# Layer 1's attention: transposing the probabilities one row of scores later

## The chip, the cores and the metric

The kernel runs on one core of a Trainium2 chip. Its engines work side by side, each through its own queue of instructions: TensorE (PE in the profile; its weight loads are listed as PEld), VectorE (DVE), ScalarE (ACT), GpSimd (POOL) and SyncE (SP, which here only issues transfers). The metric is the device time of one execution in microseconds (us); lower is better.

## The reference

Four layers, each of which adds an attention-like part and a feed-forward part to the residual x. All is float32. The change is in layer 1's attention, a latent attention with 16 heads over 4 sequences of 512 tokens. Cut to what matters:

```python
q = _rmsnorm(x @ wq_a, q_a_ln_w) @ wq_b              # 16 heads of 128 + 64
ckv = x @ wkv_a                                       # 64 latent + 64 rotary
kv = _rmsnorm(compressed_kv, kv_a_ln_w) @ wkv_b
q_pe, k_pe = rotary(q_pe), rotary(k_pe)
scores = jnp.einsum('bqhd,bkhd->bhqk', qf, kf) * softmax_scale
scores = jnp.where(causal, scores, finfo.min)
attn = jax.nn.softmax(scores, axis=-1)
out = jnp.einsum('bhqk,bkhd->bqhd', attn, v).reshape(b, s, -1) @ wo
...
x = x + _L1_attn_ref(xn, ...) + _L1_ffn_ref(xn, ...)
```

Layer 1's feed-forward part is a product-key lookup (512 experts, 8 gathered for each token) plus a gated MLP of width 1024.

## The kernel before

**Streams woven together.** A layer is written as several Python generators. Each emits some instructions and then yields an estimate of what they cost; `weave` always resumes the generator that is least advanced in relation to its total. In layer 1 these are the attention (`latent_pieces`, total 457), the product-key lookup (237, mostly DVE, POOL gathers and ACT), the gated MLP (126, mostly PE) and, from late on, the first part of layer 2. The framework then schedules the woven program: the order written is a priority, and an instruction that its estimate takes to be ready may be issued ahead of one that is not. Instructions wrapped in `keep_in_program_order` are pinned behind the previous one written for the same engine. The framework also adds all semaphores, and lets a tile wait until the buffer it reuses is free.

**The attention.** One step `s` of the loop stands for one head of one sequence; there are 64, and two neighbours make a pair. Each has four rows of scores, `i` = 0 to 3, of 128 queries against 128, 256, 384 and 512 keys (the causal half).

- `probabilities(s, i)` emits one row: the score matmul (L1042, two instructions), the masked reduction on DVE (L1045), the exponential on ACT with its row sum (L1049). After row 2 the sums of rows 0 to 2 are inverted on DVE (L1165) and the three rows scaled on ACT (L1167), after row 3 the last row. The rows `pr0` to `pr3` have two buffers each.
- `turned(s, j)` emits piece j of the transposed probabilities (L1174): the blocks of key block j from rows j to 3, so 4, 3, 2 and 1 transposes on PE, into a PSUM bank of the tag "tr", which has two banks. The copy out of the bank into `PT` (L1178) is returned as a function, and emitted after the next piece: on DVE for j = 0 and 2 (512 and 256 columns), on ACT for j = 1 and 3 (384 and 128). `PT` has two buffers, one for each head of a pair.
- The values' product `z` of a pair of heads (L1328): 16 matmul calls of 64 output rows, pinned in order, which read both heads' `PT`. ACT copies it scaled to `zT` (L1334, three buffers).
- `out_pieces` (L1282): after every second pair, the product with the output weights, in two pieces, which are emitted after row 1 and row 3 of the next odd step, and added to x on DVE (L212).
- `queries(p)` (L1129 to L1134, and with new weights of a group of heads L1103 to L1117) emits the next pair's projected queries at row 0 of an even step, with the exchange of halves through four transfers `psw<-pes` on SP (L1139). `rotate` (L1148 to L1151) emits their rotation on DVE at row 0 of an odd step.

PSUM has four banks of tag "mm" (scores, projections, the MLP), two of "tr", and two of "acc" (z, output products).

In source order, step s emits for each i: score row i of head s, transposes T(i) of head s - 1, copy of T(i - 1). At the end of the step comes the last copy, and at the end of an even step z of the pair s - 2, s - 1. So with the row number in brackets:

```
odd s:   row(0) T(0) | row(1) T(1) out | row(2) T(2) | row(3) T(3) out
even s:  row(0) T(0) queries | row(1) T(1) | row(2) T(2) | row(3) T(3) z
```

where the output pieces stand only in every fourth step. Step 64 has no scores and finishes the last pair.

Of the kernel before, what the change touches and what calls it, by code (L numbers as in the profile page):

```python
# [16 lines left out]
P = 128  # L17
NB, SEQ, DM = 4, 512, 256
NT = NB * SEQ
NTILE = NT // P  # L20
TPB = SEQ // P
# [1013 lines left out]
def exp_scores(c, pool, late, q, k, i, total, scale=1.0, kept=lambda ins: ins, **kw):  # L1035

    nc = c.nc
    n = (i + 1) * P  # L1040
    sc = c.ps()[:, :n]
    kept(nc.tensor.matmul(sc, lhsT=q[:, i * P : n], rhs=k[:, :n], start=True, stop=True))  # L1042
    pr = c.tile(pool, [P, n], f"pr{i}", **kw)
    nm = c.tile(pool, [P, 1], "nm", bufs=4)
    nc.vector.tensor_tensor_reduce(  # L1045
        out=pr, in0=sc, in1=late[:, SEQ - n :], scale=scale, scalar=-NEG,
        op0=ALU.add, op1=ALU.min, accum_out=nm,
    )
    nc.scalar.activation(pr, pr, AF.Exp, bias=nm, scale=-1.0, accum_out=total)  # L1049
    return pr  # L1050
# [20 lines left out]
def latent_pieces(c, a, keep, open_pool):  # L1071
# [20 lines left out]
    pool = open_pool()  # L1092
    weights = {}

    def carry(g):

        w = c.unit(a["l_units"][g])
        wqT, wkT, wvT = v3(w[:, :768], QL), v3(w[:, 768:1024], KL), v3(w[:, 1024:1280], KL)
        wo = v3(w[:, 1792:2816], DM)
        pw, pv = c.ps(), c.ps()  # L1100
        for h in range(4):
            hk = slice(h * KL, (h + 1) * KL)
            nc.tensor.matmul(pw[:, hk], lhsT=wqT[:, h, :P], rhs=wkT[:, h, :], start=True, stop=True)  # L1103
            nc.tensor.matmul(
                pv[(h % 2) * KL : (h % 2 + 1) * KL, (h // 2) * DM : (h // 2 + 1) * DM],
                lhsT=wvT[:, h, :], rhs=wo[:, h, :], start=True, stop=True,
            )
        pw1 = c.ps()
        for h in range(4):
            hk = slice(h * KL, (h + 1) * KL)  # L1110
            nc.tensor.matmul(pw1[KL:, hk], lhsT=wqT[:, h, P:], rhs=wkT[:, h, :], start=True, stop=True)
        wl0 = c.tile(pool, [P, 256], "wl0")
        wl1 = c.tile(pool, [P, 256], "wl1")
        wz = c.tile(pool, [P, 2, DM], "wz")
        nc.scalar.copy(wl0, pw[:, :256])
        nc.scalar.copy(wl1[KL:, :], pw1[KL:, :256])
        nc.scalar.copy(wz, v3(pv, DM))  # L1117
        weights[g] = w[:, 1280:1536], w[:KL, 1536:1792], wl0, wl1, wz

    def queries(p):  # L1120

        g, b, pair = p // 8, p // 2 % 4, p % 2
        if p % 8 == 0:
            carry(g)
        wpe0, wpe1, wl0, wl1, _ = weights[g]
        tokens = slice(b * SEQ, (b + 1) * SEQ)
        cols = slice(pair * P, (pair + 1) * P)
        pe, pl = c.ps(), c.ps()
        nc.tensor.matmul(pl, lhsT=wl0[:, cols], rhs=qa0[:, tokens], start=True, stop=False)  # L1129
        upper = nc.tensor.matmul(pe, lhsT=wpe1[:, cols], rhs=qa1[:KL, tokens], start=True, stop=False)  # L1130
        with tc.issue_after(upper.ins), tc.high_priority(offset=200):
            nc.tensor.matmul(pl, lhsT=wl1[KL:, cols], rhs=qa1[KL:, tokens], start=False, stop=True)
        with tc.high_priority(offset=100):
            nc.tensor.matmul(pe, lhsT=wpe0[:, cols], rhs=qa0[:, tokens], start=False, stop=True)  # L1134

        pes, psw = (c.tile(pool, [P, SEQ], n, bufs=1) for n in ("pes", "psw"))
        nc.scalar.copy(pes, pe)
        for to in range(0, P, 32):
            nc.sync.dma_start(psw[to : to + 32, :], pes[to ^ 32 : (to ^ 32) + 32, :])  # L1139
        qf = c.tile(pool, [P, 2, SEQ], "qf")  # L1140
        nc.scalar.mul(qf[:KL, 0, :], pl[:KL, :], -scale)
        nc.scalar.mul(qf[KL:, 1, :], pl[KL:, :], -scale)
        qfs[p] = qf
        return pes, psw, qf

    def rotate(pes, psw, qf):
        pec = c.tile(pool, [P, SEQ], "pec", bufs=1)
        nc.vector.tensor_mul(pec, pes, cosq)  # L1148
        tc.keep_in_program_order(nc.vector.tensor_mul(psw, psw, sinq))
        nc.vector.tensor_add(qf[:KL, 1, :], pec[:KL, :], psw[:KL, :])  # L1150
        nc.vector.tensor_add(qf[KL:, 0, :], pec[KL:, :], psw[KL:, :])  # L1151

    def probabilities(s, i):
        p, h = s // 2, s % 2
        b = p // 2 % 4
        if i == 0:
            totals[s] = c.tile(pool, [P, TPB], "total")
        rinv = totals[s]
        prs[s].append(exp_scores(
            c, pool, late, qfs[p][:, h, :], kf[:, h, b * SEQ : (b + 1) * SEQ], i, rinv[:, i : i + 1]  # L1160
        ))
        if i >= TPB - 2:

            done = slice(0, i + 1) if i < TPB - 1 else slice(i, i + 1)
            nc.vector.reciprocal(rinv[:, done], rinv[:, done])  # L1165
            for j in range(TPB)[done]:
                nc.scalar.mul(prs[s][j], prs[s][j], rinv[:, j : j + 1])  # L1167

    def turned(s, j):

        pt = c.ps("tr")
        n = SEQ - j * P
        for i in range(j, TPB):
            nc.tensor.transpose(  # L1174
                pt[:, (i - j) * P : (i - j + 1) * P], prs[s][i][:, j * P : (j + 1) * P], c.ident
            )
        copy = nc.scalar.copy if j % 2 else nc.vector.tensor_copy
        return lambda: copy(PTs[s][:, START[j] : START[j] + n], pt[:, :n])  # L1178

    START = (0, 512, 896, 1152)  # L1180
    qfs, prs, totals, PTs, zTs = {}, {}, {}, {}, {}
# [84 lines left out]
    turning = queries(0)  # L1266
# [8 lines left out]
    def out_pieces(g, b):  # L1275

        wz, parts = weights[g][4], zTs.copy()
        for t in range(0, TPB, 2):
            po = v3(c.ps("acc"), DM)
            for j in range(2):  # L1280
                for k in range(2):
                    nc.tensor.matmul(  # L1282
                        po[:, j, :], lhsT=parts[k][:, (t + j) * P : (t + j + 1) * P],
                        rhs=wz[:, k, :], start=(k == 0), stop=(k == 1),
                    )
            add_pair(c, b * TPB + t, po)
            if g == 3 and t == TPB - 2:
                c.part_done(b)
            yield 1.7

    copy, pieces = None, iter(())
    yield 1.9
    for s in range(65):
        if s < 64:
            prs[s] = []
        for i in range(TPB):
            if s < 64:
                probabilities(s, i)
            if s > 0:
                if i == 0:  # L1300
                    PTs[s - 1] = c.tile(pool, [P, 1280], "PT")
                ready, copy = copy, turned(s - 1, i)
                if ready:
                    ready()
            if i == 0 and s % 2 == 1 and s < 63:
                rotate(*turning)
            yield 0.85
            if i % 2:
                yield from islice(pieces, 1)
            if i == 0 and s % 2 == 0 and s < 62:  # L1310
                turning = queries(s // 2 + 1)
                yield 2.6
        if copy:
            copy()
            copy = None
        if s > 0:
            del prs[s - 1]
        if s % 2 == 1:
            continue
        if s == 0:  # L1320
            continue

        p = s // 2 - 1
        g, b, pair = p // 8, p // 2 % 4, p % 2
        z = c.ps("acc")
        for j in range(TPB):
            for h in range(2):
                tc.keep_in_program_order(nc.tensor.matmul(  # L1328
                    z[h * KL : (h + 1) * KL, j * P :], lhsT=cv[:, b * TPB + j, :],
                    rhs=PTs[s - 2 + h][:, START[j] : START[j] + SEQ - j * P],  # L1330
                    start=(j == 0), stop=(j == TPB - 1),
                ))
        zTs[pair] = c.tile(pool, [P, SEQ], "zT", bufs=3)
        nc.scalar.mul(zTs[pair], z, kv_w)  # L1334
        yield 2.1
        if pair == 1:
            pieces = out_pieces(g, b)
# [1176 lines left out]
```

## Time and profile before

| what | value |
|---|---|
| time, median of 3 runs | 2913.95 us (2909.5 to 2915.22) |
| the profiled execution | 2915.69 us |
| its span, first to last instruction | 2913.9 us |
| mean granted TensorE clock | 0.996 |
| layer 1's heads, first transposes to last | 857 to 1457 us |
| in these 600 us: PE busy | 582.8 us, with 2703 matmul instructions |
| PEld, DVE, ACT, POOL busy | 340.6, 486.6, 410.3, 120.8 us |
| transposes L1174 | 640 instructions, 124.9 us busy |
| scalings L1167 on ACT | 256, 123.5 us |
| copies L1178 on DVE and on ACT | 128 of 550 ns and 128 of 361 ns |

All times inside an execution are microseconds from the first instruction. In a group line, "x4" counts instructions, and in brackets stands how long the engine was idle before and what released it. Matmuls are pipelined: the recorded duration of one overlaps the next, so PE's busy time says little about how densely it works, and the distance from start to start says more. A line number is that of the instruction in the listing above.

### The profile page before, as it was taken

To read this page: it belongs to the slowest core of one execution; us is meant where nothing else is said; L and a number is where in the kernel's file an instruction comes from. 1 tells how busy PE (TensorE), PEld (TensorE's weight loads), DVE (VectorE), ACT (ScalarE), POOL (GpSimd) and SP (SyncE) were. 2 spreads that over 40 slices of the span, in tenths; PEclk is the share of its full clock that TensorE was granted. 3 is DMA by queue.
4 is the path that set the end of the run, shared out by engine and by line. 5 is a ranking of instruction groups with operands and counts; after the bars stand their busy time and mean duration, and the time that the engine had idled before them with its cause. 6 is when DMAs were issued, how large, how long until landed. Compare 5 with 4: busy or idle time off the path is not lost.

```text
span 2913.9 us, 40511 instructions
## 1 busy us (share of the span) xinstructions
PE 2860.2 (98%) x13767; PEld 1920.8 (66%) x13767; DVE 2131.7 (73%) x5421; ACT 1401.9 (48%) x3354; POOL 862.4 (30%) x687
## 2 busy tenths in 40 slices
PE   9999999999999999999999999999999999999999
PEld 5566665666655655555577688888888756666666
DVE  6778778787778787888775687777777666666666
ACT  4444445454366666667733554444444333333332
POOL 0565655656510033333035100000000043333331
PEclk9999999999999999999999999999999999999999
DMA  2433333333320144444234544444444300000000
GB/s 106 119 109 115 113 98 95 109 116 97 109 82 17 54 101 124 116 107 112 79 120 120 164 118 125 144 130 130 147 124 141 102 1 22 22 22 22 22 1 30
DMA packets 138687, 268.60 MB, mean 92 GB/s; under 512 B 19729, under 2 KB 99105, under 8 KB 134129
## 3 DMA queue, kind: packets, MB, share of 16 engines
q1 hardware_dynamic: 124016, 218.20, 24.4%
q0 software_dynamic: 14176, 47.04, 6.5%
q8 instruction: 109, 1.79, 0.3%
q14 instruction: 98, 0.79, 0.1%
q10 hardware_dynamic: 288, 0.79, 0.1%
HBM read 202.25 MB, written 54.26 MB: 88 GB/s over the span
## 4 chain that ended last, share of the span: by engine, by line
PE 59%; DVE 7%; ACT 4%; DMA 2%; issue 1%; SPq 0%; POOL 0%; DVEq 0%; ACTq 0%
PE mm L358 17%; PE acc L358 7%; PE mm L1042 6%; PE tr L358 6%; PE acc L1709 5%; PE acc L1058 4%; PE mm L177 3%; PE acc L266 1%; PE acc L1328 1%; DVE pr L1045 1%; PE tr L1174 1%; ACT pr L1049 1%; PE mm L185 1%; PE mm L2121 1%; ACT pr L1167 1%
## 5 line engine op out<-in xcount | busy, mean ns | idle before, releaser
L1049 ACT ACTIVATE pr<-pr,nm 128x128 f32<-128x128 f32 (+3 forms) x512 | 286.4, 560 | 297.6 <-DVE nm L1045 293.4
L1045 DVE CUSTOM_DVE_ANT_0 pr<-mm,late 128x128 f32<-128x128 f32 (+3 forms) x512 | 246.0, 483 | 115.9 <-PE mm L1042 114.3
L177 PE MATMUL mm<-xnT,wu 128*128 128x512 f32 x624 | 283.2, 595 | 0.9 <-DVE cy L620 0.5
L369 ACT COPY part<-mm 128x512 f32<-128x512 f32 (+1 forms) x372 | 177.9, 479 | 210.8 <-PE mm L358 202.6
L358 PE MATMUL mm<-token_sums,unit_sums 128*128 128x512 f32 (+1 forms) x624 | 268.1, 512 | 3.6 <-ACT part L369 3.6
L1435 POOL DMA_INDIRECT e<-in_p_experts,ids x128 | 127.7, 998 | 463.7 <-DVE x L206 358.3
L177 PE MATMUL mm<-xnT,w_in 128*128 128x512 f32 x512 | 230.9, 594 | 2.8 <-DVE cy L620 2.8
L520 DVE SCALAR_TENSOR_TENSOR x<-acc,cw,x 128x128 f32<-128x128 f32 x372 | 128.7, 346 | 106.8 <-PE acc L358 105.1
L177 PEld LDWEIGHTS mm<-xnT,wu 128*128 128x128 f32 x624 | 115.4, 190 | 126.6 <-issue 117.9
L620 DVE SCALAR_TENSOR_TENSOR cy<-mm,ws,cy 128x509 f32<-128x509 f32 (+2 forms) x216 | 159.8, 744 | 40.9 <-ACT cy L616 37.1
L1042 PE MATMUL mm<-kf,qf 128*128 128x128 f32 (+3 forms) x512 | 180.2, 443 | 3.8 <-DVE nm L1045 1.9
L785 ACT ACTIVATE xD<-xc,ws 128x128 f32<-128x128 f32 x256 | 83.6, 390 | 193.3 <-POOL y L826 182.8
L802 POOL TENSOR_TENSOR G<-G,CB 128x1024 f32<-128x1024 f32 x64 | 151.1, 2361 | 76.8 <-DVE G L765 76.8
L1042 PE MATMUL mm<-k,q 128*128 128x128 f32 (+3 forms) x512 | 170.5, 438 | 2.6 <-DVE nm L1045 2.3
L358 PEld LDWEIGHTS acc<-down_sums,hidden_sums 128*128 128x128 f32 x744 | 111.7, 191 | 85.1 <-issue 83.4
L177 PEld LDWEIGHTS mm<-xnT,w_in 128*128 128x128 f32 x512 | 95.8, 190 | 107.2 <-issue 91.8
L1709 PEld LDWEIGHTS acc<-PT,V 128*128 128x128 f32 x1280 | 153.8, 193 | 5.1 <-issue 1.7
L1709 PE MATMUL acc<-PT,V 128*128 128x128 f32 x1280 | 153.9, 276 | 0.0
L302 POOL TENSOR_TENSOR down_sums<-wu 128x256 f32<-128x256 f32 x8 | 5.8, 730 | 498.4 <-DMA wu<-in_o_units 498.4
L765 DVE TENSOR_TENSOR_SCAN G<-G,eye 128x1024 f32<-128x1024 f32 x64 | 147.2, 2300 | 0.1
L1174 PEld LDWEIGHTS tr<-con,pr 128*128 128x128 f32 x640 | 82.3, 141 | 89.9 <-ACT pr L1167 26.7
L503 DVE TENSOR_TENSOR whole<-mm,part 128x512 f32<-128x512 f32 x128 | 88.5, 692 | 68.9 <-PE mm L358 68.9
(456 smaller groups left out, 6735.1 us busy)
## 6 DMA issues: line engine op xcount, KB each, us to landing
turned<-Y SPq DMA_DIRECT2D x252, 160.0 KB, 2.6
PT<-turned SPq DMA_DIRECT2D x63, 640.0 KB, 3.9
G<-own SPq DMA_DIRECT2D x64, 512.0 KB, 4.7
w_in<-in_m_units SPq DMA_DIRECT2D x16, 1024.0 KB, 5.9
eb<-since SPq DMA_DIRECT2D x96, 128.0 KB, 3.5
wu<-in_o_units SPq DMA_DIRECT2D x6, 1536.0 KB, 6.6
wo<-in_m_units SPq DMA_DIRECT2D x16, 512.0 KB, 4.3
psw<-pes SPq DMA_DIRECT2D x128, 64.0 KB, 2.0
```

The lines of the kernel that those rows point to most:

```text
L177: c.nc.tensor.matmul(out, lhsT=w[:, d, cols], rhs=c.xnT[:, d, tokens], start=(d == 0), stop=(d == 1))
L358: self.kept(self.c.nc.tensor.matmul(bank, lhsT=lhsT, rhs=rhs, start=first, stop=True, skip_group_check=not first))
L369: self.c.nc.scalar.copy(r, bank)
L520: c.nc.vector.scalar_tensor_tensor(x, bank, self.factor(u, tt), x, ALU.mult, ALU.add)
L620: nc.vector.scalar_tensor_tensor(y[:, j:], src[:, : SEQ - j], conv[:, k, 3 - j : 4 - j], y[:, j:], ALU.mult, ALU.add,)
L765: tc.keep_in_program_order(nc.vector.tensor_tensor_scan(flat, flat, eye.rearrange("p h t -> p (h t)"), 0.0, ALU.mult, ALU.add))
L802: nc.gpsimd.tensor_mul(G, G, seqs[b][2][:, t, :][:, None, :].to_broadcast([P, HG, P]))
L1042: kept(nc.tensor.matmul(sc, lhsT=q[:, i * P : n], rhs=k[:, :n], start=True, stop=True))
L1045: nc.vector.tensor_tensor_reduce(out=pr, in0=sc, in1=late[:, SEQ - n :], scale=scale, scalar=-NEG, op0=ALU.add, op1=ALU.min, accum_out=nm,)
L1049: nc.scalar.activation(pr, pr, AF.Exp, bias=nm, scale=-1.0, accum_out=total)
L1435: nc.gpsimd.indirect_dma_start(out=e, out_offset=None, in_=a["p_experts"], in_offset=bass.IndirectOffsetOnAxis(ap=ids[:, t, k : k + 1], ax ...
L1709: kept(nc.tensor.matmul(zs[:, i], lhsT=head["V"][:, j, h, :], rhs=head["PT"][:, :, i * (i + 1) // 2 + j, :], start=(j == 0), stop=(j == i),))
```

## The change

The loop over heads and rows is flattened: n counts rows of scores, s = n // 4 and i = n % 4. A row of scores is emitted at its n as before. Piece j of head `done` is emitted at n = 4 done + j + 5 instead of 4 done + j + 4: one row of scores later. The values' product of a pair follows its last piece, as before, and so now comes after row 0 of the next odd step instead of at the end of the even one. Queries, rotation and output pieces keep their places among the rows.

```diff
-    for s in range(65):
+    for n in range(4 * 65 + 1):
+        s, i = divmod(n, TPB)
         if s < 64:
-            prs[s] = []
-        for i in range(TPB):
-            if s < 64:
-                probabilities(s, i)
-            if s > 0:
-                if i == 0:
-                    PTs[s - 1] = c.tile(pool, [P, 1280], "PT")
-                ready, copy = copy, turned(s - 1, i)
-                if ready:
-                    ready()
-            if i == 0 and s % 2 == 1 and s < 63:
-                rotate(*turning)
-            yield 0.85
-            if i % 2:
-                yield from islice(pieces, 1)
-            if i == 0 and s % 2 == 0 and s < 62:
-                turning = queries(s // 2 + 1)
-                yield 2.6
-        if copy:
-            copy()
-            copy = None
-        if s > 0:
-            del prs[s - 1]
-        if s % 2 == 1:
+            if i == 0:
+                prs[s] = []
+            probabilities(s, i)
+        done, j = divmod(n - TPB - 1, TPB)
+        if done >= 0:
+            if j == 0:
+                PTs[done] = c.tile(pool, [P, 1280], "PT")
+            ready, copy = copy, turned(done, j)
+            if ready:
+                ready()
+        if i == 0 and s % 2 == 1 and s < 63:
+            rotate(*turning)
+        yield 0.85
+        if i % 2:
+            yield from islice(pieces, 1)
+        if i == 0 and s % 2 == 0 and s < 62:
+            turning = queries(s // 2 + 1)
+            yield 2.6
+        if done < 0 or j < TPB - 1:
             continue
-        if s == 0:
+        copy()
+        copy = None
+        del prs[done]
+        if done % 2 == 0:
             continue
 
-        p = s // 2 - 1
+        p = done // 2
...
-                    rhs=PTs[s - 2 + h][:, START[j] : START[j] + SEQ - j * P],
+                    rhs=PTs[done - 1 + h][:, START[j] : START[j] + SEQ - j * P],
```

In source order it then reads, with T of the head before and, in brackets, its piece:

```
odd s:   row(0) T(3) z | row(1) T(0) out | row(2) T(1) | row(3) T(2) out
even s:  row(0) T(3) queries | row(1) T(0) | row(2) T(1) | row(3) T(2)
```

where T(3) at row 0 still belongs to head s - 2.

## The prediction

> **What bounds the kernel now.** I read the page first: engine totals, clock row, chain.
>
> ```profile
> PE 2860.2 (98%) x13767; PEld 1920.8 (66%) x13767; DVE 2131.7 (73%) x5421; ACT 1401.9 (48%) x3354; POOL 862.4 (30%) x687
> PE 59%; DVE 7%; ACT 4%; DMA 2%; issue 1%; SPq 0%; POOL 0%; DVEq 0%; ACTq 0%
> ```
>
> TensorE (PE) is the bound, and the chain that ended last runs mostly through it. But 98% is not a full engine: matmuls overlap, so a short wait hides inside the recorded durations. What counts is the time from one start to the next. The timeline of one row of scores in layer 1 gives the price list:
>
> ```profile
> 1105.62 0.60 PE L1174 MATMUL tr<-con,pr 128*128 128x128 f32 x4
> ...
> 1106.06 0.60 PE L1042 MATMUL mm<-kf,qf 128*128 128x256 f32 x2
> ...
> 1106.49 0.49 PE L1174 MATMUL tr<-con,pr 128*128 128x128 f32 x3
> ...
> 1106.82 0.81 PE L1042 MATMUL mm<-kf,qf 128*128 128x384 f32 x2
> ...
> 1107.55 0.20 PEld L1174 LDWEIGHTS tr<-con,pr 128*128 128x128 f32 x2 [0.54 <-ACT PT L1178]
> ```
>
> Four transposes take 1106.06 - 1105.62 = 0.44 us (0.11 each), two 256-column matmuls 0.43, three transposes 0.33. So 128 columns cost 0.109 us, and score rows 0 to 3 cost 0.22, 0.43, 0.65 and 0.87. Taking every matmul between 857 and 1457 us this way, I counted what its start came later than that price: the 640 transposes of L1174 lose 24.5 us. The largest releaser, ending 0.05 us before the start, is the scaling L1167 with 13.2 us in 43 places; the copies out of PSUM, L1178, come to 8.2 us in 20; 3.1 us have no clear one. The view of waits agrees in order:
>
> ```profile
> PEld tr L1174 <- ACT pr L1167: 26.7, 67, 2.0
> PEld tr L1174 <- issue: 23.1, 101, 0.8
> PEld tr L1174 <- ACT PT L1178: 12.6, 20, 2.0
> PEld tr L1174 <- DVE PT L1178: 9.3, 18, 1.0
> ```
>
> These are idle times of the weight loader, partly under running matmuls, so upper bounds; the same view for PE itself has 5.3 us for L1167 and 4.9 us for L1178, the lower bounds. One wait did more. Busy times and granted clock by windows:
>
> ```profile
> 1120.00:1127.00 7.00, 7.00 (x27) 4.41 (x26) 5.71 (x16) 1.94 (x7) 2.01 (x2) 1.00 0.25 67
> 1127.00:1130.80 3.80, 2.03 (x12) 1.33 (x10) 3.80 (x12) 2.14 (x7) 1.20 (x2) 1.00 0.32 81
> 1130.80:1137.60 6.80, 6.80 (x25) 4.06 (x26) 3.48 (x13) 2.24 (x7) 4.22 (x5) 0.50 0.65 172
> ```
>
> (window, us, then PE, PEld, DVE, ACT, POOL busy, clock, DMA.) PE was 2.03 us busy of 3.80, ending with 1.50 us idle for L1167, and then ran 6.8 us at clock 0.50: 3.4 us of work lost.
>
> **The change, part by part.** No arithmetic, tile or DMA is added or removed. I write Tj for the transposes of piece j (4, 3, 2, 1 of them). Only their place in source order moves: T0 from behind score row 0 to behind row 1, T3 behind the next head's row 0; the product z with it. The trace shows that issue order is not source order: the projections L1129 (written behind T0) start at 1109.02, T0 at 1112.00. So the move shifts priorities, and some of it is done already.
>
> *T0 and T1 against L1167.* T0 needs the last row's chain: reduce, exp, reciprocal, four scalings. At 1107.83 row 3 starts, its issue ends 0.87 later at 1108.70, the scalings end at 1112.25: 3.55 us. One head later the same is 1114.97 to 1118.72, 3.75 us. PE work in between, by source, into an odd row of heads (z is there, 2.30 us from 1115.16 to 1117.46): before, T3 0.11 + z 2.30 + row 0 0.22 = 2.63; after, T2 0.22 + row 0 0.22 + T3 0.11 + z 2.30 + row 1 0.43 = 3.28, and the last of T0's four sits 0.33 later, 3.61. Into an even row: before 0.33 by source (the scheduler pulled projections in); after, 0.22 + 0.22 + 0.11 + projections 2.9 (1109.02 to 1111.9) + 0.43 = 3.88. Both reach the chain's length. Of 13.2 us I take away 8: each place gains at least row 1's 0.43, some waits are longer (1.50, and groups of 0.6 to 0.8). Bounds: 0 (the scheduler had already filled) and 13.2.
>
> *T2 against its PSUM bank.* Two banks take turns, so T2 waits for T0's copy. PE work between their starts, less T0's own 0.44: before 0.43 + 0.33 + 0.65 = 1.41, after 0.65 + 0.33 + 0.87 = 1.85. Of 8.2 us I take 3 away; bounds 0 and 8.2.
>
> *T3 against T1's copy on ACT.* Here the cover shrinks: before 0.65 + 0.22 + 0.87 = 1.74, after 0.87 + 0.22 + 0.22 = 1.31. The copy takes 0.48. A loss of 2 us (64 places, a few tenths in some); bounds 0 and the rival below. T0's own bank gains z or the projections as cover.
>
> *z one piece later; its reader does not move.* The output pieces (L1282) stay at rows 1 and 3 of the next odd head, so z's copy zT now has only row 1 0.43 + T0 0.44 ahead of the first piece, plus 0.43 for that piece's half that reads the other pair. ACT did this:
>
> ```profile
> 1115.16 2.38 PE L1328 MATMUL acc<-PT,cv 128*64 128x512 f32 x16
> ...
> 1116.82 1.90 ACT L1167 ACTIVATE pr<-pr,total 128x128 f32<-128x128 f32 x4
> ...
> 1118.63 0.67 ACT L1334 ACTIVATE zT<-acc,kv_w 128x512 f32<-128x512 f32 x1
> ```
>
> zT ended 1119.30 - 1117.46 = 1.84 us behind z, because the four scalings stood in front. Against 1.30 of cover this is short by 0.5, in 16 places 8 us if nothing else fills; the rest of the row (0.65 + 0.33) is there to fill. I take 2 lost; bounds 0 and 8. Behind a waiting output piece PE's queue stands still: rows 2 and 3 of scores, then DVE and ACT with them. DVE's pair addition behind it is waited for by nobody near.
>
> *Clock.* The 1.50 us wait stood before T0 of an odd head with new group weights (L1103, L1104) still to do; the change puts those ahead of T0. I take 3.4 back; bounds -3.4 and +3.4 (one new dip elsewhere). The Trainium skill, "TensorE: Matmul & The Clock Gate", section "Why this matters for your kernels", has the clock fall only after idle gaps of about 3 us; here 1.50 us, in a stretch 2.03 of 3.80 busy, went before it. By the page the clock term is 0, by the row 3.4, and the measurement decides.
>
> *One more step of the loop* (n = 256 holds no scores): 0.85 of planner cost, no instruction; the tail holds T's and z with little beside them. +0.4, bounds 0 and 0.85. *Queues:* SP's psw<-pes transfers follow the projections, which do not move against score rows; POOL's gathers wait for DVE additions of another stream. Nothing on SP or POOL is moved past another; 0. *Buffers:* a row's probabilities are last read three pieces instead of four before their buffer returns, still after PE has passed; 0.
>
> Another rule speaks against the change: the Trainium skill, "Perfetto Trace Analysis", section "Optimization Strategy", says that a gap that repeats can mean too few buffers in SBUF or PSUM. If all waits were the banks', an order with the same two banks would give about 0. The rows put only 8.2 of 24.5 us there, so I go by 13.2 us for the scalings.
>
> Sum: -8 - 3 + 2 + 2 - 3.4 + 0.4 = -10.0 us. Against the profiled span 2913.9 that is 2903.9; that execution took 2915.69, 1.8 outside its span and 1.7 above the median of the runs, 2913.95. The forecast for the median is 2904; its own range, from the bounds that are likely together, 2894 to 2911.
>
> **The rivals.**
>
> *Slower: T1's copy gets stuck behind the scalings.* Four scalings occupy ACT for 1.9 us. If the copy of T1 is put behind them, T3 starts 1.9 + 0.48 + 0.2 = 2.6 us behind T1 against 1.31 of cover: 1.3 lost. z, pinned behind T3, waits too. It decides from about 12 of 64 heads (16 us lost against the 12 won, T3's 2 now counted here). At 20 heads: +26 - 12 = +14, 2928; at 14 heads about 2920. For it: ACT copies already hold T's for 12.6 us in 20 places, up to 2.0. Against it: the scheduler places copies before exponentials that come ready later (a 384 copy at 1107.02, between rows 0 and 1). Chance 0.22.
>
> *No difference: the scheduler had done it.* Projections and other streams already fill; T0's waits reappear one row later since the estimate of ACT that caused them is the same. 2914, give or take 4. For it: L1129 ahead of T0. Against it: 43 places remain. Chance 0.2.
>
> *More:* all 24.5 us of the transposes' waits and the clock's 3.4 go: 2914 - 28 = 2886. Against it: the two banks stay. Chance 0.06.
>
> **How the numbers follow.** The forecast, 0.52, is the likeliest, and its time is the prediction. The range must leave out no more than 2 in 10: down to 2893, up to 2921, which holds the no-difference rival and the mild half of the slower one; what it leaves out is the rest of that one and the last rival. A measurement of this kernel tells about 0.2%, 5.8 us, from no change. Faster than 2908.1: most of the forecast (0.50) and the last rival (0.06), 0.56. Within: the second rival and the forecast's rest, 0.20. Slower: the first rival and the no-difference case's upper edge, 0.24.
>
> **What would show it.** L1174's waits for L1167 fall from 26.7 to under 12; those for DVE's L1178 shrink, for ACT's L1178 grow a little; L1282 begins to wait for L1334; clock 1.00 around 1130; layer 1's last z some 10 us earlier, and everything behind it shifted alike. Wrong if the L1174 waits for ACT copies exceed 25 us, if a new window with clock 0.50 stands between 860 and 1440, or if the time goes in layer 2 or 3.

## The result: about 6 us slower, in a range that had it, with the wrong sign

| | before | after |
|---|---|---|
| median of 21 runs each | 2913.42 us (2907.43 to 2916.93) | 2919.23 us (2914.48 to 2927.43) |
| ratio after to before | | 1.0022 [1.0016, 1.0028] |
| the profiled execution, and its span | 2915.69, 2913.9 us | 2915.68, 2913.9 us |

The forecast was 2904. The range, 2893 to 2921, held the result only because its upper part was left open for two rivals; what happened is the working of neither, so that is luck. The two profiled executions happen to have the same span: before's is among the longer of its runs, after's among the shortest of its own. Totals of the two profiles can't show the 6 us; what is read below is where each loses time, and the medians say what the difference is. Behind the loop, line numbers of after are one lower: the values' product z is L1327, its copy zT L1333.

The page of after, engine totals and the chain that ended last:

```profile
PE 2854.4 (98%) x13767; PEld 1922.4 (66%) x13767; DVE 2130.5 (73%) x5421; ACT 1405.2 (48%) x3354; POOL 864.1 (30%) x687
...
PE 60%; DVE 5%; ACT 4%; DMA 2%; issue 1%; SPq 1%; DVEq 0%; ACTq 0%
```

The same instructions with the same bound: a change of order alone. The view of waits of after, 845 to 1470 us (total, times, longest), and two rows of the same view of before:

```profile
PEld tr L1174 <- DVE PT L1178: 16.9, 26, 2.1
PEld tr L1174 <- ACT PT L1178: 10.3, 15, 2.7
PEld tr L1174 <- ACT pr L1167: 7.2, 20, 0.8
PE acc L1327 <- DVE PT L1178: 4.2, 3, 2.3
PE tr L159 <- ACT xnT L164: 3.7, 2, 3.0
PE tr L159 <- DVE PT L1178: 3.3, 2, 3.1
```

```profile
PE tr L159 <- ACT PT L1178: 1.2, 1, 1.2
PE acc L1328 <- DVE PT L1178: 0.2, 1, 0.2
```

The wait that the change was aimed at fell from 26.7 to 7.2, as forecast. But DVE's copies rose from 9.3 to 16.9, and two waits of PE grew from next to nothing: z's for copies on DVE (0.2 to 4.2), and those of the transposes of layer 2's normalised input (L159; 1.2 to 7.0), which share the two "tr" banks.

Counted by starts, as in the prediction (0.109 us for 128 columns, what is later than that is lost; half-clock stretches taken out of all but the transposes' split):

| lost by, us (layer 1 from 845 us to layer 2's first expert matmul) | before | after |
|---|---|---|
| T's for the scalings L1167 | 13.2 (43 places) | 4.6 (19) |
| T's for ACT's copies L1178 | 5.1 (10) | 5.2 (11) |
| T's for DVE's copies L1178 | 4.9 (12) | 7.5 (14) |
| z | 5.7 | 10.0 |
| layer norm's transposes L159 | 1.7 | 9.0 |
| all matmuls | 66.7 | 69.0 |

The prediction's own count gave the two rows of copies 8.2 us in 20 places; this one, over a slightly longer stretch, gives them 10.0 in 22, and it is the one used for every kernel below. The rows say where the waits moved. They do not add up to the 6 us: all matmuls lose only 2.3 us more.

z's new wait, in the timeline of after (start, duration, instruction; in brackets the idle time before). First PE, then DVE:

```profile
1174.99 0.38 PE L1174 MATMUL tr<-con,pr 128*128 128x128 f32 x2
1175.21 0.39 PE L1042 MATMUL mm<-kf,qf 128*128 128x128 f32 x2
1175.43 0.27 PE L1174 MATMUL tr<-con,pr 128*128 128x128 f32 x1
1175.63 2.15 PE L1327 MATMUL acc<-PT,cv 128*64 128x512 f32 x10
1180.06 0.86 PE L1327 MATMUL acc<-PT,cv 128*64 128x256 f32 x6 [2.28 <-DVE PT L1178]
```

```profile
1176.69 0.69 DVE L220 SCALAR_TENSOR_TENSOR sg<-sg,mm 128x512 f32<-128x512 f32 x1 [0.90 <-ACT sg L219]
1177.56 0.69 DVE L1149 TENSOR_TENSOR psw<-psw,tab 128x512 f32<-128x512 f32 x1 [0.18 <-DMA psw<-pes]
1178.17 0.68 DVE L221 SCALAR_TENSOR_TENSOR hT<-sg,mm 128x512 f32<-128x512 f32 x1
1178.77 0.68 DVE L1045 CUSTOM_DVE_ANT_0 pr<-mm,late 128x512 f32<-128x512 f32 x1
1179.38 0.28 DVE L1045 CUSTOM_DVE_ANT_0 pr<-mm,late 128x128 f32<-128x128 f32 x1
1179.59 0.42 DVE L1178 COPY PT<-tr 128x256 f32<-128x256 f32 x1
```

T2 is done at 1175.37 and z reaches its 11th instruction at 1177.78 (z has 8 matmul calls of two instructions each; the 11th is the first that reads the later head's copy of T2). The copy of T2, 0.42 us long, starts only at 1179.59: five DVE instructions stand ahead of it, the first of which waited 0.90 for ACT and the second 0.18 for a transfer. Before the change score row 3 (0.87) lay between T2 and z; now it is row 0 (0.22).

The layer norm's wait, same view:

```profile
1402.69 0.63 PE L159 MATMUL tr<-con,xn 128*128 128x128 f32 x4 [0.18 <-DVE PT L1178]
1406.34 0.66 PE L159 MATMUL tr<-con,xn 128*128 128x128 f32 x4 [3.02 <-ACT xnT L164]
```

```profile
1402.83 0.71 ACT L1049 ACTIVATE pr<-pr,nm 128x512 f32<-128x512 f32 x1
...
1403.53 1.90 ACT L1167 ACTIVATE pr<-pr,total 128x128 f32<-128x128 f32 x4
1405.34 0.38 ACT L1049 ACTIVATE pr<-pr,nm 128x128 f32<-128x128 f32 x1
...
1405.72 0.56 ACT L164 COPY xnT<-tr 128x512 f32<-128x512 f32 x1
```

The bank that the second group needs is freed by a copy that ACT does behind an exponential, the four scalings and another exponential. PE stood for 3.02 us and paid twice, as the windows show (length, PE, PEld, DVE, ACT, POOL busy, clock, DMA share, GB/s):

```profile
1403.40:1406.34 2.94, 0.00 (x1) 0.01 (x1) 0.16 (x1) 2.94 (x10) 0.00 (x0) 1.00 0.68 212
1406.90:1410.40 3.50, 3.50 (x25) 1.61 (x26) 2.06 (x3) 0.96 (x2) 0.00 (x0) 0.55 0.00 0
```

Before's half-clock stretch at 1130 is gone as forecast, and this one stands in after, with another behind the 3.09 us wait at 1446. (Before's profile has two there as well, at 1445 and 1469, so single profiles don't say which kernel has more.) A new stretch between 860 and 1440 is one of the signs of being wrong that the prediction listed. The last matmul of the last z starts 2.0 us later than before (1461.06 against 1459.05), where some 10 us earlier was forecast.

Taken by halves, with half of each half-clock stretch taken off, heads 0 to 31 take 301.9 us in place of before's 304.8, and heads 32 to 63 take 298.4 in place of 291.9. In a second profile of the change (set 2 below) it is 301.5 and 295.4. The change gains 3 us in the first half and loses 3.5 to 6.5 in the second.

### The profile page after: what moved, and what is told of

Its sections match the earlier page's. It is cut to its first block, busy times and chain, and to the rows that moved or that the text cites. A ratio compares the mean times of both kernels' runs of the same rounds, so it can differ in the third digit from the quotient of the medians.

```text
span 2913.9 us, 40517 instructions
## 1 busy us (share of the span) xinstructions
PE 2854.4 (98%) x13767; PEld 1922.4 (66%) x13767; DVE 2130.5 (73%) x5421; ACT 1405.2 (48%) x3354; POOL 864.1 (30%) x687
## 4 chain that ended last, share of the span: by engine, by line
PE 60%; DVE 5%; ACT 4%; DMA 2%; issue 1%; SPq 1%; DVEq 0%; ACTq 0%
PE mm L358 17%; PE mm L1042 7%; PE acc L358 7%; PE tr L358 6%; PE acc L1708 5%; PE acc L1058 4%; PE mm L177 3%; PE acc L266 2%; DMA psw<-pes 2%; PE acc L1327 2%; PE tr L1174 1%; PE acc L1282 1%; PE mm L2120 1%; PE mm L185 1%; ACT pr L1049 1%
```

## The experiments

All runs of a set share one chip and the runs of the kernel before made there; ratios are to those. Four sets.

**Set 1: is it z, the pieces, DVE's copies, or the plan as such?** Before's median in this set is 2908.45. The times in the expectations were named against 2913, so a result is to be held against them by its ratio: the four ratios below, times 2913.42, are 2918.7, 2917.8, 2916.6 and 2916.0 us.

*z yet one row later* (after, with z emitted behind score row 1 and ahead of T0):

```diff
             probabilities(s, i)
+        if product:
+            yield from product(done)
+            product = None
         done, j = divmod(n - TPB - 1, TPB)
...
-        z = c.ps("acc")
...
+        product = values
```

> The changed kernel, with the values' product z of a pair one more row later (behind score row 1, ahead of T0). Theory A (z now stands too close behind the copy of T2 on VectorE; in the changed kernel's profile z's own waits grew from 5.9 to 11.5 us): z's waits fall back to about 6 us, and the time from 2919 to 2912 to 2915. Theory B (the loss is in the layer norm's transposes of layer 2, L159, which share the two PSUM banks, 2.7 to 9.4 us): z's waits fall, but the time stays at 2916 to 2920. Theory N (any new plan of the scheduler moves the time by a few us, no cause): anything from 2910 to 2924, unrelated to z's waits.

2914.96 us, 1.0018 [1.0009, 1.0027]. z's wait for T2's copy fell from 4.9 to 1.9 us, but z lost 9.4 in all, in many small places, and T's waits for scalings came to 6.6. Little is regained: a row of distance more for z moves its wait rather than ending it. By its ratio the run fits theory B's 2916 to 2920, though z's waits hardly fell in all.

*The pieces late, z where it was* (before, with no piece behind row 0, T0 behind row 1, T1 behind row 2, T2 and T3 behind row 3):

```diff
-                if i == 0:
-                    PTs[s - 1] = c.tile(pool, [P, 1280], "PT")
-                ready, copy = copy, turned(s - 1, i)
-                if ready:
-                    ready()
+                for j in ((), (0,), (1,), (2, 3))[i]:
+                    if j == 0:
+                        PTs[s - 1] = c.tile(pool, [P, 1280], "PT")
+                    ready, copy = copy, turned(s - 1, j)
+                    if ready:
+                        ready()
```

> The kernel before, with T0 and T1 one row later and T2 as there, T3 right behind T2 in row 3: z and its reader keep the old places. Theory A: the scalings' waits (L1167) fall from 13 us to about 5 without z's loss, time 2905 to 2910 against 2913 of before. Theory B: depends on where L159 falls; 2906 to 2916. Theory N: anything from 2908 to 2922. If it is slower than 2914 although L1167's waits fell and z's did not grow, theory A falls.

2913.59 us, 1.0015 [1.0006, 1.0024]. The scalings' share falls to 3.1 us in 9 places, the lowest of the set, and DVE's copies take 13.9 and z 8.7. Not faster either: the gain on the scalings is paid back at the banks and at z. The edit doesn't free z, though. z keeps its place, but T2, whose copy it reads, now stands right ahead of T3 and z, without row 3 (0.87) between, and z loses 8.7 where before lost 5.7. So the run doesn't tell the pieces' share from z's.

*DVE's and ACT's copies ahead of other work* (after):

```diff
-        return lambda: copy(PTs[s][:, START[j] : START[j] + n], pt[:, :n])
+        def copied():
+            with tc.high_priority(offset=100):
+                copy(PTs[s][:, START[j] : START[j] + n], pt[:, :n])
+        return copied
```

> The changed kernel, with all copies of the transposed pieces out of PSUM (L1178) planned at a higher priority, so that VectorE and ScalarE take them ahead of rotation and other streams. Theory A: z's waits of 11.5 us fall under 7, the transposes' waits for banks too; 2911 to 2916. Theory B: 2916 to 2920. Theory N: 2910 to 2924.

2912.26 us, 1.0011 [1.0002, 1.0020], against 1.0022 for the change unaltered. z's wait for T2's copy is 0.7 us instead of 4.9 (z 5.2 in all), ACT's copies 2.4 instead of 5.2, and the scalings 8.7 instead of 4.6. With the copies early about half of the loss is left, though the two intervals overlap ([1.0016, 1.0028] for the change) and the edit also makes a new plan. What the copies gain comes partly out of the scalings, which lose 4.1 us more.

*A control that changes no order in the source* (before):

```diff
-            yield 0.85
+            yield 0.84
```

> The kernel before, with the attention's yield of 0.85 set to 0.84: no part of the change, only a slightly different interleaving of the streams. Theories A and B: 2911 to 2916, within 0.1% of before. Theory N: as far from 2913 as the change is, 2907 or 2919.

2913.92 us, 1.0009 [1.0000, 1.0018]. A hundredth in the estimate of a row's cost shifts how the streams are woven, and that alone gave four tenths of the change's effect, with an interval that just reaches down to none. Its waits:

```profile
PEld tr L1174 <- ACT pr L1167: 25.7, 64, 1.5
PEld tr L1174 <- ACT PT L1178: 13.0, 20, 1.5
PEld tr L1174 <- DVE PT L1178: 10.0, 17, 1.0
```

Much the same as before's three rows: the pattern of waits stays with the order when the plan changes.

**Set 2: the layer norm's bank, and the change once more.** Before's median is 2910.27.

*The change, unaltered:*

> The changed kernel once more, beside the kernel before on one chip, with the clock of every run of both. The earlier comparison gave a ratio of 1.0022. Theory S (the move saves the scalings' waits, and pays more for z's wait for the copy of T2, for the layer norm's transposes, and for dips of the clock): ratio 1.0015 to 1.0028; taking the clock's loss (2914 times one less the mean clock) off the spans leaves the changed kernel 2 to 6 us behind, and the clock itself costs it 1 to 5 us more. Theory N (luck of the plan alone): the same ratio, but no part of it repeats in the same places.

2916.32 us, 1.0022 [1.0012, 1.0032]: the same ratio in another set. The same places wait again: PE is idle 2.07 us ahead of z at 1177, and 3.02 and 3.10 us ahead of L159. Theory N's claim that no place repeats fell; but the program is the same one, so this doesn't speak against luck of its plan. Over its runs the mean granted clock, times the span, makes a loss of 10.8 us against before's 8.0. Of the 6 us, then, 2.8 are clock and 3.7 work at full clock.

*Layer norm's transposes in the "mm" banks instead* (after):

```diff
-        c.parts(3, lambda b: layernorm(c, b, halves[b // 2][b % 2 * SEQ : (b % 2 + 1) * SEQ, :]))
+        c.parts(3, lambda b: layernorm(c, b, halves[b // 2][b % 2 * SEQ : (b % 2 + 1) * SEQ, :], apart=True))
```

> The changed kernel, with the layer norm's transposes behind layer 1 (L159) in the four general PSUM banks and the second half two planner steps later, instead of in the two banks of the attention's transposes. Theory S: L159's waits fall from 9 us to 2 or 3 and a dip of the clock near 1407 goes, so ratio to before 1.0000 to 1.0014 (3 to 6 us better than the changed kernel). If the ratio stays at 1.0020 or more, the layer norm is no part of the cause.

2917.72 us, 1.0025 [1.0016, 1.0034]. No gain, and by the expectation's own line the layer norm's place in the shared banks is then no part of the cause. PE's stalls stayed near where they were, somewhat shorter, and named others: 2.36 us ahead of a T at 1405 for ACT's copy, 2.38 ahead of L159 at 1442 for DVE. In after's stall at 1403.40 ACT was busy for all of the 2.94 us; that ACT's load makes PE stall there whoever waits for it fits this, but no run took that load away.

*Both edits together, on after and on before:*

> The changed kernel with both cures: copies out of PSUM planned at a higher priority, and the layer norm's transposes in the general banks. Theory S: both losses gone and the saving of the scalings' waits (13 to 5 us) left over: ratio 0.997 to 1.000. Theory N: near 1.001, as the copies alone (1.0011).

> The kernel before with the same two cures, without the move: what they bring by themselves. Theory S: little, ratio 0.999 to 1.001, and 3 to 8 us slower than the changed kernel with both. Theory N: either side of it, 0.998 to 1.002.

2912.91 us, 1.0010 [1.0002, 1.0019], and 2911.12 us, 1.0003 [0.9994, 1.0012]. With copies early and the norm apart, z loses 5.5 and 4.9 us, the scalings 10.6 and 16.3. The change then costs the difference of the two ratios, 0.07%, which these runs can't tell from nothing. Theory S had the first at 0.997 to 1.000 and missed: taking both waits for the cause of the loss, and the scalings' saving for what is left, was wrong.

**Set 3: half of the heads.** In this set every kernel took longer, before 2945.63 us. Two of them were run again in set 4, and their profiles show where: 8.6 and 10.4 us more in heads 32 to 47, and 13.2 and 9.2 us more in layer 2's experts. Only ratios are used, and since what was slow lies partly in the heads that are compared, they need not hold elsewhere.

```diff
+    held = range(32)
+    steps = {}
+    for d in range(64):
+        for j in range(TPB):
+            steps.setdefault(4 * d + j + 4 + (d in held), []).append((d, j))
```

The pieces listed under `steps[n]` are emitted behind score row n: one row late for the heads in `held`, as before for the others. The second kernel has `range(32, 64)`, the third is the first with the copies early.

> The move for heads 0 to 31 alone; heads 32 to 63 keep the old places. Theory S: the first half's heads take 3 to 4 us less than in the kernel before, as in the changed kernel's profile (start of head 0 to start of head 32, the clock's loss taken off: 299.8 against 303.8), and the second half loses nothing, so ratio 0.9980 to 0.9995. Theory N (the order of a new plan is a draw, whatever half): 0.9990 to 1.0020.

> The move for heads 32 to 63 alone. Theory S: heads 0 to 31 as before, the second half as in the changed kernel (head 32 to the end of layer 1 longer by 5 to 7 us): ratio 1.0020 to 1.0040. Theory N: 0.9990 to 1.0020.

> The move for heads 0 to 31 alone, with the copies out of PSUM planned at a higher priority in all heads. Theory S: the best of all, ratio 0.9970 to 0.9990. Theory N: 0.9990 to 1.0020.

Ratios 0.9981 [0.9972, 0.9991], 1.0005 [0.9996, 1.0014] and 0.9973 [0.9963, 0.9984]. The halves make -0.19% and +0.05%; the whole made +0.22% in other sets and wasn't run in this one. The first and the third came as theory S had them. The second half has both L159 waits of after (3.0 and 3.1 us), the first has neither; yet it isn't the 0.20% to 0.40% slower that theory S had named. A price per head would add up, and these don't; with the whole measured elsewhere, that is a hint and not shown.

*A second control* (before, `yield 0.86`):

> A second control: the kernel before with the attention's yield of 0.85 set to 0.86, no part of the change. The first control gave 1.0009. Theory S: 0.9995 to 1.0010, the scatter of a new plan, less than half of the change's 1.0022. Theory N: up to 1.0025.

1.0035 [1.0023, 1.0047]: a number that means nothing for the order costs more than the change, and more than either theory had allowed.

**Set 4: the change under three plans.** Before's median is 2909.41, on the chip of set 3. `yield` 0.84 and 0.86 in after, 0.86 in before once more, and the third half-kernel again:

> The changed kernel with the attention's yield of 0.85 set to 0.84: the move with another, neutral plan. Theory S (the move itself costs about 6 us net): ratio to before 1.0015 to 1.0035, 0.1 to 0.25% above the kernel before with 0.84 (1.0009). Theory N (the plan's draw decides, the move costs nothing by itself): anywhere from 0.9985 to 1.0020, and z's wait for the copy of T2 not 4 to 5 us.

> The changed kernel with the yield set to 0.86. Theory S: slower than the kernel before with 0.86 in this same call by 0.1 to 0.25%. Theory N: as likely faster than it as slower.

> The kernel before with the yield set to 0.86 once more; the first time, on a chip on which the kernel before itself took 2946 us, it gave 1.0035. If a neutral plan can cost that much by itself (theory N), it gives 1.002 to 1.004 again; if that was this chip, 0.9995 to 1.0015.

> The move for heads 0 to 31 alone with the copies planned at a higher priority, once more on another chip (0.9973 before). Theory S: 0.9970 to 0.9990. Theory N: 0.9990 to 1.0015.

2911.56 us, 1.0005 [0.9996, 1.0014]; 2923.40 us, 1.0047 [1.0034, 1.0061]; 2921.78 us, 1.0046 [1.0032, 1.0059]; 2907.94 us, 0.9992 [0.9983, 1.0001]. The last stood at 0.9973 in set 3; the two intervals just touch at 0.9983 and 0.9984, so whether it beats the kernel before is not settled; theory N's range has it, theory S's doesn't.

All three plans side by side, without and with the change; lost us from one profile each, counted as above:

| row's estimate | ratio to before | T's for scalings | T's for copies | z | all matmuls |
|---|---|---|---|---|---|
| 0.84 | 1.0009, 1.0005 | 13.0, 4.6 | 10.2, 14.8 | 5.0, 5.8 | 64.9, 63.4 |
| 0.85 | 1, 1.0022 | 13.2, 4.6 (4.4) | 10.0, 12.7 (12.2) | 5.7, 10.0 (9.1) | 66.7, 69.0 (65.9) |
| 0.86 | 1.0046, 1.0047 | 12.8, 1.8 | 9.9, 18.8 | 5.4, 5.7 | 70.7, 69.9 |

(In brackets the second profile of the change, from set 2.) The waits of the change with 0.86 and of before with 0.86:

```profile
PEld tr L1174 <- DVE PT L1178: 19.6, 26, 3.7
PEld tr L1174 <- ACT PT L1178: 16.4, 19, 2.4
PEld tr L1174 <- ACT pr L1167: 4.6, 13, 0.8
```

```profile
PEld tr L1174 <- ACT pr L1167: 29.4, 78, 1.4
PEld tr L1174 <- ACT PT L1178: 13.7, 19, 2.0
PEld tr L1174 <- DVE PT L1178: 8.0, 13, 1.3
```

and of the change with 0.84:

```profile
PEld tr L1174 <- DVE PT L1178: 20.8, 26, 3.3
PEld tr L1174 <- ACT PT L1178: 10.3, 15, 2.2
PEld tr L1174 <- ACT pr L1167: 7.2, 15, 1.5
```

The same exchange stands three times: the scalings' row falls by some 70 to 85% (26.7 to 7.2, 25.7 to 7.2, 29.4 to 4.6), DVE's row about doubles (9.3 to 16.9, 10.0 to 20.8, 8.0 to 19.6). The change by itself makes -0.04%, +0.22% and +0.01% in the three plans, and +0.07% with both edits; each difference is uncertain by 0.1 to 0.2%, and the two ratios with 0.84 come from two chips. Theory S, that the move itself costs about 6 us, had named 0.1 to 0.25% for 0.84 and 0.86 and fell in both. Nor does the gain in the first 32 heads stand (one profile each, half of each half-clock stretch taken off as before): with 0.84 the change takes 302.3 us there in place of 298.8, with 0.86 303.1 both times; in the other 32 it takes 292.7 in place of 296.1, and 297.1 in place of 297.6.

## Why the prediction was wrong

In the terms of its sum, forecast and found (with 0.85):

| term | forecast, us | found, us |
|---|---|---|
| T0 and T1 for L1167 | -8 | -8.6 |
| T2's bank (DVE's copies) | -3 | +2.6 |
| T3's bank (ACT's copies) | +2 | +0.1 |
| z | +2, for its reader L1282 | +0.4 to 0.8 there, +4.3 at z itself |
| clock | -3.4 | +2.8 (set 2) |
| layer norm's transposes L159 | no term | +7.3 |

What is found adds up to more than the 6 us. The other matmuls lost less than before, and where exactly they gained was not followed up.

**T0 and T1 against L1167: right.** Forecast -8 us; measured -8.6 (13.2 to 4.6), and -8.4 and -11.0 in the other plans. The view of waits went under 12, as listed.

**T2 against its PSUM bank: the step that failed.** It was costed -3, with bounds 0 and 8.2, because the rows of scores between T0 and T2 are longer now. Bounds that leave out a loss need a reason, and there was none: cover was counted in PE's time, with DVE's copy taken as due when it had been due. By source order the PE work between them was to grow from 1.41 to 1.85 us. In the traces the time between them didn't grow: at the median T2 starts 2.55 us after T0's last transpose, in place of 3.09 (2.58 in place of 3.17 with 0.84, 3.11 in place of 3.22 with 0.86), and the mean, which the long waits hold up, stays between 3.3 and 3.5. This fits a PE that no longer stands for the scalings and so comes to the bank sooner. DVE doesn't come sooner: it was busy for 486.6 of the 600 us of this stage, and it starts T0's copy later, on average 1.64 us after T0's last transpose begins in place of 1.32, and more than 3 us after it in 14 heads in place of 5 (1.58 for 1.30 and 1.66 for 1.58 us in the other plans). What T2 loses where T0's copy ended less than 0.2 us before its start rose from 6.4 to 8.4 us, with 0.84 from 6.4 to 13.5, with 0.86 from 5.8 to 14.7. The two bank terms together, T2's and T3's, were forecast at -1 (-3 + 2); all copies' waits rose by 2.7, and in the plans with 0.84 and 0.86 by 4.6 and 8.9.

**T3 against T1's copy: small.** Forecast +2; ACT's copies cost 0.1 more with 0.85, 0.5 with 0.84, 3.6 with 0.86. The row of waits for ACT's copies with 0.85 is 10.3, below before's 12.6, so the slower rival, T1's copy stuck behind the scalings, did not take place; the bound of 25 that would have shown it is far off.

**z one piece later: the wrong operand.** The term priced the reader behind z (L1282 for zT; forecast +2, found 0.4 to 0.8 in the count) and not what z itself reads. z follows T3 directly, and T2's copy, on DVE, now has score row 0 ahead of z in place of row 3: 0.65 us less cover. That cost z 4.3 us in the plan with 0.85, and 0.8 and 0.3 in the others. Early copies nearly end z's wait at T2's copy (4.9 to 0.7 us), so what z waited for is shown for this plan. What that wait is worth in time isn't: the same edit moves all copies. And it isn't a necessity of the change.

**Clock: the place right, the sum wrong.** The stretch at 1130 went, and others came behind new waits; the mean loss over the runs of set 2 rose by 2.8 us where -3.4 was forecast (bounds ±3.4). The further step of the loop (+0.4) can't be told apart in these runs.

**What was not in the sum: the plan.** The prediction says of the no-difference rival "The scheduler had done it". In size that rival is the nearest over the three plans: what is lost over all matmuls moves by -1.5, +2.3 (-0.8 in the second profile) and -0.8 us. Its mechanism isn't what happened, for T0's waits didn't come back one row later; they went, and waits for the next late engine came in their place. The 6 us on top, with 0.85, repeat in two sets and belong to this plan. Of its waits, z behind a DVE queue and the layer norm's transposes (L159) stand out, but the edits aimed at them took away half of the loss at most, so that they make the 6 us is not shown. An edit of the source that makes the framework schedule anew has a scatter of its own, and the controls show its size: 0.09% and 0.46% for a hundredth of a planner's microsecond. The prediction's chances did not allow for this scatter.

**What stays open.** What the 6 us with 0.85 consist of: 2.8 are clock, and of the 3.7 at full clock the count of starts accounts for 2.3 in one profile and for none in the other. Why the plan with 0.86 costs 0.46% with either order: the runs of before with 0.86 take 5.9 us more at full clock and have a clock loss of 14.0 us against 7.4, and no single place was found. Why the kernels took 30 to 36 us longer in set 3 than in set 4. And whether the change for half of the heads with early copies is faster.

## What to carry to other kernels

When a wait of the bound engine is removed, cost the next one it will meet: for every operand of the moved instruction and every buffer it takes, name the engine that delivers it, how busy that is in this stage, and allow for a loss there. On a kernel whose order a scheduler makes, run two or three neutral changes of a planner's number first; an effect of a few tenths of a per cent is a property of the order only if it stands in all of those plans.

## What the runs showed of the hardware

The clock fell to half for 3.41 us or a multiple of it (the last stretch of an execution can have another length), at places that change from run to run of one kernel: at 786, 1407, 1448, 2285 and 2912 us in one profile of after, at 1402, 1443, 2283 and 2911 in the other. Over 21 runs of after the mean clock lies between 0.993 and 0.998, and the span follows it as 2907 + 2605 x (1 - clock) us. A stretch of 3.41 us takes 0.0006 off the mean clock and so goes with about 1.5 us.

How long PE stood idle doesn't by itself say whether such a stretch follows. In after two of them stood behind idle times of 3.02 us (1407) and 3.09 us (1448), in before four behind 1.00 us (786), 1.50 us (1130), 1.18 us (1445) and 2.15 us (1469); none stood behind 2.28 us (1180) and 1.88 us (1334) in after. The Trainium skill, "TensorE: Matmul & The Clock Gate", section "Why this matters for your kernels", names idle gaps of about 3 us; those two in after agree with it, the four in before came after shorter ones.

The same kernel on the same chip took 2945.63 us in one set of runs and 2909.41 in another, 1.2% apart; a comparison across sets would have shown that and nothing else.
